# Pairwise products of every row: one form of VectorE instruction, inputs loaded in a ring, and four longer output pieces in place of five

## The chip, the core and the metric

The kernel runs on one core of one Trainium2 chip. The metric is the device time of one execution in microseconds. TensorE has no work here: VectorE and ScalarE multiply, and the 16 DMA engines of the core bring the input in from device memory and write the output back.

## The reference

For each of 4096 rows of 256 float32 numbers, the reference forms all products of two elements of the row and keeps the upper triangle, diagonal included, in row order: 256 + 255 + ... + 1 = 32,896 products.

```python
dot = jnp.einsum('bi,bj->bij', inputs, inputs)
iu, ju = jnp.triu_indices(d)
return dot[:, iu, ju]
```

The input is 4.19 MB, the output 539 MB. One output row is a run of segments: segment i holds element i times elements i to 255, and is 256 - i long.

## The kernel before

Each of the 128 partitions holds 32 rows of the input. The loop over `groups` (16 rounds, index `g`) takes `REPEAT` = 2 rows per partition at a time. Each round's 32,896 output columns are cut by `even_borders` into `PIECES` = 5 pieces of 6528 or 6592 columns. A piece is computed into a slot `o` of the pool `opool`, which has three slots of 2 x 6592 floats per partition, and is then written out by one transfer on the SyncE queue (line 164), in packets of one row of a piece: 6592 floats, 26,368 bytes, two for each partition. A new piece can be computed into a slot only when the transfer that read it has landed.

The very first piece of the kernel is cut further, at `FIRST` = 512, 1536 and 3584 columns, so that output can begin early: it goes out as four transfers.

The input is loaded at the start into one tile `xt` that stays for the whole kernel (line 120), in three transfers of 256, 1792 and 2048 KB (line 124).

Inside a piece, `runs` lists the segments that lie in it. `split` gives the first `k` of them to ScalarE, as one activation (line 137) for each segment and each of the two rows, with the scale read from the input; it stops when VectorE's estimated time for the rest is within `BUDGET` = 1.08 ns per element of the piece, or when ScalarE would take longer than VectorE. In the first piece the budget is 0, so the two engines share the work evenly. VectorE does the rest in one of three ways that `vector_ops` chooses by estimated cost:

- "each": one tensor_scalar per row (line 149), at 130 ns + 0.52 ns per element, twice;
- "all": one tensor_tensor over both rows (line 158), with the scalar operand repeated by a stride of 0;
- "two": one tensor_tensor over both rows and two neighbouring segments. The second segment is one element shorter than the first, so this instruction writes one column too many, which the next segment then overwrites. The input tile has one spare element at its end, cleared by a memset, for reads that run over.

```python
each = REPEAT * (130 + 0.52 * n)
together = 68 + 1.046 * REPEAT * n - (34 if two else 0)
```

`interleave` orders VectorE's instructions of a piece so that they come alternately from its two halves, and `vector_time` adds up the estimates. The Tile layer adds the semaphores and decides the order in which instructions stand on each engine. All transfers, loads and outputs, are issued from one queue, SyncE's, in that order.

Of the kernel before, what the change touches and what calls it, by code (L numbers as in the profile page):

```python
# [1 line left out]

# [4 lines left out]

F32 = mybir.dt.float32
AF = mybir.ActivationFunctionType
ALU = mybir.AluOpType  # L10

P = 128
UNIT = 64
REPEAT = 2
PIECES = 5
BUDGET = 1.08
FIRST = [512, 1536, 3584]


def even_borders(lo: int, hi: int, pieces: int) -> list[int]:  # L20
    units = (hi - lo) // UNIT
    return [lo + units * c // pieces * UNIT for c in range(pieces)] + [hi]


def runs(d: int, lo: int, hi: int) -> list:


    found, at = [], 0
    for i in range(d):
        a, b = max(at, lo), min(at + d - i, hi)  # L30
        if a < b:
            found.append((i, i + a - at, a, b - a))
        at += d - i
    return found


def vector_ops(block: list) -> list:

    ops, k = [], 0
    while k < len(block):
        i, j, at, n = block[k]
        two = k + 2 < len(block) and i == j
        each = REPEAT * (130 + 0.52 * n)
        together = 68 + 1.046 * REPEAT * n - (34 if two else 0)
        if each <= together:
            ops.append(("each", block[k]))  # L50
        elif two:
            ops.append(("two", block[k]))
            k += 1
        else:
            ops.append(("all", block[k]))
        k += 1
    return ops


def interleave(block: list) -> list:  # L60


    half = len(block)
    while half and len(vector_ops(block[:half])) > len(vector_ops(block[half:])):
        half -= 1
    a, b = vector_ops(block[:half]), vector_ops(block[half:])
    return [op for k in range(max(len(a), len(b))) for ops in (a, b) for op in ops[k : k + 1]]


def vector_time(block: list) -> float:  # L70
    t = 0.0
    for way, (i, j, at, n) in vector_ops(block):
        if way == "each":
            t += REPEAT * (130 + 0.52 * n)
        else:
            t += 68 + 1.046 * REPEAT * n * (2 if way == "two" else 1)
    return t


def split(block: list, budget: float) -> int:  # L80


    scalar, k = 0.0, 0
    while k < len(block):
        scalar += REPEAT * (184 + 0.837 * block[k][3])
        if vector_time(block[k:]) <= budget or scalar > vector_time(block[k + 1 :]):
            break
        k += 1
    return k


def window(ap: bass.AP, free: list) -> bass.AP:
    return bass.AP(ap.tensor, ap.offset, [list(ap.ap[0]), *free])


@with_exitstack
def kernel(
    ctx: ExitStack, tc: tile.TileContext, x: bass.AP, out: bass.AP
):

    nc = tc.nc
    n, d = x.shape
    width = out.shape[1]
    assert n % (P * REPEAT) == 0 and width == d * (d + 1) // 2 and width % UNIT == 0
    groups = n // (P * REPEAT)
    borders = even_borders(0, width, PIECES)
    slot = max(b - a for a, b in zip(borders, borders[1:]))  # L110

    xpool = ctx.enter_context(tc.tile_pool(name="x", bufs=1))
    opool = ctx.enter_context(tc.tile_pool(name="o", bufs=3))

    x_in = x.rearrange("(p r) d -> p (r d)", p=P)
    x_out = out.rearrange("(p g r) c -> g p r c", p=P, r=REPEAT)


    total = n // P * d
    xt = xpool.tile([P, total + 1], F32, name="x")  # L120
    nc.vector.memset(xt[:, total:], 0.0)  # L121
    cuts = [0, REPEAT * d, total // 2, total]
    for a, b in zip(cuts, cuts[1:]):
        nc.sync.dma_start(xt[:, a:b], x_in[:, a:b])

    for g in range(groups):
        for c, (lo, hi) in enumerate(zip(borders, borders[1:])):
            o = opool.tile([P, REPEAT, slot], F32, tag="o", name=f"o_{g}_{c}")
            first = g == c == 0
            cuts = [lo, *(FIRST if first else []), hi]  # L130
            for a, b in zip(cuts, cuts[1:]):
                block = runs(d, a, b)
                k = split(block, 0.0 if first else BUDGET * REPEAT * (b - a))
                for i, j, at, length in block[:k]:
                    for r in range(REPEAT):
                        row = (g * REPEAT + r) * d
                        nc.scalar.activation(  # L137
                            o[:, r, at - lo : at - lo + length],
                            xt[:, row + j : row + j + length],
                            AF.Copy,  # L140
                            scale=xt[:, row + i : row + i + 1],
                        )
                row = g * REPEAT * d
                for way, (i, j, at, length) in interleave(block[k:]):
                    at -= lo
                    if way == "each":
                        for r in range(REPEAT):
                            row_r = row + r * d
                            nc.vector.tensor_scalar(  # L149
                                o[:, r, at : at + length],  # L150
                                xt[:, row_r + j : row_r + j + length],
                                xt[:, row_r + i : row_r + i + 1],
                                None,
                                ALU.mult,
                            )
                        continue
                    m = 2 if way == "two" else 1
                    nc.vector.tensor_tensor(  # L158
                        o[:, :, at : at + m * length],
                        window(xt[:, row + j :], [[d, REPEAT], [1, m], [1, length]]),  # L160
                        window(xt[:, row + i :], [[d, REPEAT], [1, m], [0, length]]),
                        ALU.mult,
                    )
                nc.sync.dma_start(x_out[g][:, :, a:b], o[:, :, a - lo : b - lo])  # L164


# [1 line left out]
_INS = ["r_inputs"]  # L168
_OUTS = [((4096, 32896), "float32")]


# [20 lines left out]
```

## Time and profile before

The median of three runs is 1277.83 us (1277.81 to 1277.97). The profiled execution has a span of 1276.1 us from its first to its last instruction.

| What | Value |
|---|---|
| VectorE busy | 1128.9 us, 88% of the span |
| ScalarE busy | 234.7 us, 18% |
| tensor_tensor, line 158 | 1651 instructions, 804.2 us, mean 559 ns |
| tensor_scalar, line 149 | 1326 instructions, 344.9 us, mean 333 ns |
| activation, line 137 | 786 instructions, 233.4 us, mean 384 ns |
| DMA packets | 23,040, mean 426 GB/s over the span |
| memory read, written | 4.19 MB, 538.97 MB |
| an output transfer, issue to landing | 33.0 us (median of 64 of 6592 KB) |

How to read it: busy times are those of one engine and overlap with those of the others. The duration of an instruction reaches into that of the next on VectorE, so a stretch of back-to-back instructions is shorter than the sum of their durations; where a text speaks of a pitch, it means the time from one start to the next. "Issue to landing" counts from the instruction on the queue until all 16 DMA engines have reported; with other transfers ahead in the queue it is longer than the transfer itself. The page counts 1376 of the packets under 512 bytes: these are the 16 semaphore writes of each of the 86 transfers. In views of windows, the DMA share is the time of all packets over 16 times the window, and may pass 1 where packets overlap.

### The profile page before, as it was taken

To read this page: it belongs to the slowest core of one execution; us is meant where nothing else is said; L and a number is where in the kernel's file an instruction comes from. 1 tells how busy PE (TensorE), PEld (TensorE's weight loads), DVE (VectorE), ACT (ScalarE), POOL (GpSimd) and SP (SyncE) were. 2 spreads that over 40 slices of the span, in tenths; PEclk is the share of its full clock that TensorE was granted. 3 is DMA by queue.
4 is the path that set the end of the run, shared out by engine and by line. 5 is a ranking of instruction groups with operands and counts; after the bars stand their busy time and mean duration, and the time that the engine had idled before them with its cause. 6 is when DMAs were issued, how large, how long until landed. Compare 5 with 4: busy or idle time off the path is not lost.

```text
span 1276.1 us, 4106 instructions
## 1 busy us (share of the span) xinstructions
DVE 1128.9 (88%) x2978; ACT 234.7 (18%) x787; POOL 0.2 (0%) x4
## 2 busy tenths in 40 slices
DVE  8999989898898988989889898898988989888880
ACT  4211112121121301213012130121301213012130
POOL 0000000000000000000000000000000000000000
DMA  9999999999999999999999999999999999999997
GB/s 385 433 434 430 428 432 426 433 426 433 428 430 432 427 434 423 435 426 432 428 430 431 427 435 424 434 425 434 429 430 432 426 433 424 434 428 432 430 428 314
DMA packets 23040, 543.43 MB, mean 426 GB/s; under 512 B 1376, under 2 KB 1376, under 8 KB 2016
## 3 DMA queue, kind: packets, MB, share of 16 engines
q1 hardware_dynamic: 23008, 543.17, 99.5%
q14 instruction: 32, 0.26, 0.0%
HBM read 4.19 MB, written 538.97 MB: 426 GB/s over the span
## 4 chain that ended last, share of the span: by engine, by line
DMA 62%; DVE 35%; issue 0%; DVEq 0%; SPq 0%
DMA out_dram<-o 62%; DVE o L158 24%; DVE o L149 11%; DMA x<-in_r_inputs_dram 0%; SPq L164 0%; DVEq L158 0%; DVEq L149 0%; DVEq L188 0%
## 5 line engine op out<-in xcount | busy, mean ns | idle before, releaser
L158 DVE TENSOR_TENSOR o<-x 128x104 f32<-128x104 f32 (+60 forms) x1651 | 804.2, 559 | 59.3 <-DMA out_dram<-o 59.3
L137 ACT ACTIVATE o<-x 128x197 f32<-128x197 f32 (+25 forms) x786 | 233.4, 384 | 1000.6 <-DMA out_dram<-o 892.5
L149 DVE TENSOR_SCALAR o<-x 128x216 f32<-128x216 f32 (+5 forms) x1326 | 344.9, 333 | 53.1 <-DMA out_dram<-o 50.4
L137 ACT ACT_TABLE_LOAD x1 | 1.3, 1283 | 0.7 <-PEq L179 0.7
L121 DVE MEMSET x<- 128x1 f32 x1 | 0.1, 59 | 0.8 <-PEq L179 0.8
L179 POOL MEMSET const-bfloat16-1.0<- 128x1 bf16 x1 | 0.1, 102 | 0.0
L179 POOL MEMSET const-uint8-127<- 128x1 uint8 x1 | 0.1, 102 | 0.0
L179 POOL MEMSET const-float32-0.0<- 128x1 f32 x1 | 0.1, 99 | 0.2 <-issue 0.2
L179 POOL MEMSET const-float32-1.0<- 128x1 f32 x1 | 0.1, 99 | 0.0
## 6 DMA issues: line engine op xcount, KB each, us to landing
out_dram<-o SPq DMA_DIRECT2D x64, 6592.0 KB, 33.0
out_dram<-o SPq DMA_DIRECT2D x15, 6528.0 KB, 33.3
out_dram<-o SPq DMA_DIRECT2D x1, 2944.0 KB, 16.8
x<-in_r_inputs_dram SPq DMA_DIRECT2D x1, 2048.0 KB, 12.6
out_dram<-o SPq DMA_DIRECT2D x1, 2048.0 KB, 13.8
x<-in_r_inputs_dram SPq DMA_DIRECT2D x1, 1792.0 KB, 7.1
out_dram<-o SPq DMA_DIRECT2D x1, 1024.0 KB, 11.8
out_dram<-o SPq DMA_DIRECT2D x1, 512.0 KB, 10.8
```

Of the source, the lines that this page charges most:

```text
L121: nc.vector.memset(xt[:, total:], 0.0)
L137: nc.scalar.activation(o[:, r, at - lo : at - lo + length], xt[:, row + j : row + j + length], AF.Copy, scale=xt[:, row + i : row + i + 1],)
L149: nc.vector.tensor_scalar(o[:, r, at : at + length], xt[:, row_r + j : row_r + j + length], xt[:, row_r + i : row_r + i + 1], None, ALU.mult,)
L158: nc.vector.tensor_tensor(o[:, :, at : at + m * length], window(xt[:, row + j :], [[d, REPEAT], [1, m], [1, length]]), window(xt[:, row + ...
L179: nc = _bacc.Bacc("TRN2", target_bir_lowering=False, num_devices=1)
```

## The change

Three things are changed together.

1. VectorE uses tensor_tensor only. `vector_ops` no longer weighs the three ways: two neighbouring segments are taken together wherever they have their full length in the piece, a single segment otherwise. `BUDGET` goes from 1.08 to 0.95, so `split` gives ScalarE more segments: 1420 activations in place of 786.
2. The input comes in a ring of three small tiles. Each holds `LOADED` = 2 rounds (1024 floats per partition, 512 KB in all, and the spare element, now cleared on GpSimd). Two tiles are asked for ahead of the loop, and each later one four rounds before it is used; the third of them has a buffer free from the start, and in the built program its load stands on the queue ahead of all outputs.
3. The memory this frees (32 KB per partition for the whole input against 12 KB for the ring) goes into longer slots: `PIECES` goes from 5 to 4, pieces have 8192 or 8256 columns, and packets 32,768 or 33,024 bytes.

```diff
-PIECES = 5
-BUDGET = 1.08
+PIECES = 4
+BUDGET = 0.95
+LOADED = 2
 FIRST = [512, 1536, 3584]
...
         i, j, at, n = block[k]
-        two = k + 2 < len(block) and i == j
-        each = REPEAT * (130 + 0.52 * n)
-        together = 68 + 1.046 * REPEAT * n - (34 if two else 0)
-        if each <= together:
-            ops.append(("each", block[k]))
...
+        m = 2 if k + 2 < len(block) and i == j else 1
+        ops.append((block[k], m))
+        k += m
     return ops
...
-    xpool = ctx.enter_context(tc.tile_pool(name="x", bufs=1))
+    xpool = ctx.enter_context(tc.tile_pool(name="x", bufs=3))
...
-    total = n // P * d
-    xt = xpool.tile([P, total + 1], F32, name="x")
-    nc.vector.memset(xt[:, total:], 0.0)
-    cuts = [0, REPEAT * d, total // 2, total]
-    for a, b in zip(cuts, cuts[1:]):
-        nc.sync.dma_start(xt[:, a:b], x_in[:, a:b])
+    def load(g: int):
+        size = LOADED * REPEAT * d
+        xt = xpool.tile([P, size + 1], F32, tag="x", name=f"x_{g}")
+        nc.gpsimd.memset(xt[:, size:], 0.0)
+        cuts = [0, REPEAT * d, size] if g == 0 else [0, size]
+        for a, b in zip(cuts, cuts[1:]):
+            nc.sync.dma_start(xt[:, a:b], x_in[:, g * REPEAT * d + a : g * REPEAT * d + b])
+        return xt
+
+    loaded = {g: load(g) for g in range(0, 2 * LOADED, LOADED)}
...
                 nc.sync.dma_start(x_out[g][:, :, a:b], o[:, :, a - lo : b - lo])
+            ahead = g + 2 * LOADED
+            if c == 0 and g % LOADED == 0 and ahead < groups:
+                loaded[ahead] = load(ahead)
```

## The prediction

> **What bounds the kernel now.** I read the page's parts 1 to 3 first, then the chain of waits, then windows over the last ten and the first thirty microseconds.
>
> ```profile
> DVE 1128.9 (88%) x2978; ACT 234.7 (18%) x787; POOL 0.2 (0%) x4
> ...
> DMA  9999999999999999999999999999999999999997
> ...
> q1 hardware_dynamic: 23008, 543.17, 99.5%
> q14 instruction: 32, 0.26, 0.0%
> ```
>
> The DMA row is full in every slice but the last, and the output queue is busy for 99.5% of the span: this kernel writes at the speed of its DMA engines. VectorE, at 88%, waits for them. The chain in order of time says the same:
>
> ```profile
> 613.59 13.87 DVE o L149 x54
> 627.48 33.31 DMA out_dram<-o
> 660.81 14.22 DVE o L158 x24
> ```
>
> VectorE fills a slot in about 14 us, and the transfer then takes 33 us to land, since two others stand ahead of it. Three slots turn once in 47.3 us. The chain passes 187.87 us and 1181.29 us in the same phase, 63 transfers apart: 15.768 us a transfer, on the slowest of the 16 engines. The windows at the end show that it is one engine:
>
> ```profile
> 1266.00:1267.00 1.00, 0.00 (x0) 0.00 (x0) 0.00 (x0) 1.00 0.98 422
> 1267.00:1268.00 1.00, 0.00 (x0) 0.00 (x0) 0.00 (x0) 1.00 0.25 106
> 1268.00:1269.00 1.00, 0.00 (x0) 0.00 (x0) 0.00 (x0) 1.00 0.18 79
> 1269.00:1274.00 5.00, 0.00 (x0) 0.00 (x0) 0.00 (x0) 1.00 0.06 26
> ```
>
> The last two columns are the DMA share and GB/s. A share of 0.06 is one engine of 16: most have finished near 1267.2, one works until about 1274.8. It is late by some 7 us, after the same number of output packets as the others. The row q14 explains it: 32 instruction fetches of 8 KB. In the window from 18 to 21 us, where packets of 8 KB ran alone, share 1.02 at 431 GB/s gives 16 x 8192 x 1.02 / 431 = 310 ns a packet. VectorE's 3049 instructions (semaphore steps included) at 64 bytes (0.26 MB over 4106) are 23.8 fetches, 7.4 us. I read this as VectorE's stream being fetched through one DMA engine, which therefore ends last.
>
> Finally the start:
>
> ```profile
> 3.60 10.01 ACT L137 ACTIVATE o<-x 128x253 f32<-128x253 f32 x28 [1.59 <-DMA x<-in_r_inputs_dram]
> 3.60 1.14 DVE L149 TENSOR_SCALAR o<-x 128x256 f32<-128x256 f32 x4 [2.74 <-DMA x<-in_r_inputs_dram]
> ```
> ```profile
> 6.00:9.00 3.00, 3.00 (x14) 3.00 (x10) 0.00 (x0) 1.00 0.99 424
> 9.00:12.00 3.00, 3.00 (x14) 3.00 (x11) 0.00 (x0) 1.00 1.13 355
> 12.00:14.00 2.00, 2.00 (x10) 1.61 (x5) 0.00 (x0) 1.00 0.70 257
> ```
>
> The DMA engines are busy with the 4.19 MB of input until about 13.5 us, and behind that wait output parts computed meanwhile. The load hides the start of the computation.
>
> [...] the timeline shows 0.245 us for 224 elements (17.57 to 18.06 for two) and 0.96 us for 856 (16.61 to 17.57). With its larger fixed part tensor_scalar thus costs 1.09 ns per element at this length and tensor_tensor 1.12: VectorE loses little by the exchange. [...]
>
> **The change part by part.**
>
> *Fewer, longer packets.* 83 output transfers become 67, of 16 packets per engine each: 1328 packets per engine become 1072. Price of a packet: at 27.2 bytes/ns the mean 26,317 bytes take 967.5 ns; 15.768 us / 16 is 985.5, so 18 ns are extra. Of these, 7 us / 1264 packets = 5.5 ns belong to the fetches. That leaves 12.5 ns for every packet (if part grows with bytes, 9 to 10). Saving: 256 x 12.5 = 3.2 us, at least 2.2.
>
> *VectorE by tensor_tensor only.* 3049 VectorE instructions become 1881, so 14.7 fetches instead of 23.8 on the engine that ends last: 9.1 x 0.31 = 2.8 us. ScalarE goes from 786 to 1420 activations, 11.7 fetches on, I take it, another engine, still fewer than VectorE's. In the steady state a piece costs VectorE at most 15.7 us (the code's 68 ns + 1.046 ns per element; on the block of 12,244 elements before, 14.1 by that formula against 14.19 in the chain) and ScalarE at most 12.4, while its transfer takes 16 x 1.227 = 19.6. With three slots the next output is issued some 20 us before it is needed, so both hide.
>
> *One interleaving.* The built order puts the last eight instructions of piece 3 of the first round among those of the next piece, behind a wait for the transfer of piece 1. By my times that landed before VectorE arrives there; piece 3 is issued near 67 us, needed at 72. Nothing.
>
> *The ring of loads.* Only three loads (1.5 MB, 3.7 us) stand at the head of the queue; the five others (4 KB packets) follow the outputs. The memsets on GpSimd wait for readers long done. So the start is no longer hidden. VectorE's blocks until piece 1 is finished, by the formula and the built order: 1.27 + 1.89 + 3.03 + 6.38 + 15.46 = 28.0 us. From 3.60 that is 31.6, issued at 31.8 (VectorE is the slower of the two in each block). First packet 1.0 us after the issue (the first load: issued at 0.73, bytes from 1.7); I take 1.1: 32.9. Until then the engines have 3.7 us of loads and 19.8 us of output parts (16 packets each of 2, 4, 8 and 18 KB: 84, 160, 310 and 686 ns), and begin at 1.75: they stand idle for 32.9 - 1.75 - 23.5 = 7.6 us in all, the longest stretch, over 4 us, just ahead of piece 1. Before, the same sum for piece 1 gives an issue at 27.5, with transfers queued to about 29.5: no gap.
>
> *The sum, from piece 1 on, for the slowest engine.* 512 packets of 33,024 bytes at 1226.6 ns = 628.0; 496 of 32,768 at 1217.2 = 603.7; 40 of 4 KB loads at 163 ns = 6.5, and I add 0.5 for going between reads and writes; 14.3 fetches at 0.30 = 4.3. From 32.9 this ends at 1275.9. The same sum for before (29.8 + 79 x 15.768) ends at 1275.4 where the trace has about 1274.8, so I take 0.5 off: 1275.4, that is 0.6 later than before. **The saving of packets and fetches (6 us) and what the slow bulk load cost (about 1.5) are given back at the start (7.6) and in mid-stream loads.** 1277.8 + 0.7 = 1278.5 us.
>
> **Unknown costs.** The switch between reading and writing is not in the trace of before. From below nothing (a fetch of 8 KB mid-stream, also a read, costs only its own length, 7 us / 23.8 = 0.29); from above: the bulk loads ran at 355 GB/s with one dip to 0.70 over 2 us, so 0.6 us each, 3 in all. The latency from issue to first packet: 0.9 to 1.5. The part of the packet overhead that grows with length: up to 1 us.
>
> **Rivals.**
> 1. *Slower*: mid-stream loads at their upper price, or packets over 32 KB that are cut in two (512 more at 12.5 ns, 6 us): 1281 to 1285. For it: no such packet or load is in this trace. Against: cost per packet is the same from 8 to 26 KB. Chance 0.22.
> 2. *Faster*: the start is hidden after all or the fetches weigh more than I think: without the 7.6 us, 1271; with half of it, 1274.7. For it: the ring brings compute no later than before. Against: the engines have only 3.7 us of loads, and VectorE needs 28 us for what they carry in 23.5. Chance 0.08.
> 3. *VectorE becomes the bound*: 15.7 of work and about 1.5 of landing and issue per slot against 19.6; it would need 3 us more in every piece. It would give 64 x 20 = 1280 at the least. Chance under 0.02, counted within rival 1.
>
> My forecast, no measurable change, has 0.70: it holds from 1275.3 to 1280.4. The range reaches from 2.7 us below (all price errors in favour) to 4.1 above (loads at their upper price and 1 us of longer packets).
>
> **What would show it.** A DMA row with a dip in the slices before 33 us and VectorE busy there; piece 1 issued at 31.8; steady transfers of 19.5 to 19.7 us; a lone engine at the end for 4 to 5 us instead of 7; about 28 fetches in q14 (14.7 for VectorE, 11.7 for ScalarE, the rest for the others) and 19,550 packets in all. It is wrong if the first slices are full, if the transfer takes over 19.8 us, if packets number well over 19,600, or if the outputs behind the mid-stream loads come late by more than the loads' 1.3 us.

## The result and the profile after

The changed kernel takes 1282.75 us (median of four runs, 1282.58 to 1282.82) against 1277.9 us before: a ratio of 1.0038, with a 95% interval of 1.002 to 1.0055. It is 4.9 us slower. No change had been forecast, at 1278.5 us.

The page after, its VectorE row, DMA row, queues and loads:

```profile
DVE 990.4 (77%) x1811; ACT 464.6 (36%) x1421; POOL 0.9 (0%) x12
...
DMA  7999999999999999999999999999999999999996
...
DMA packets 19548, 543.40 MB, mean 424 GB/s; under 512 B 1216, under 2 KB 1216, under 8 KB 2880
...
q1 hardware_dynamic: 19520, 543.17, 98.9%
q14 instruction: 28, 0.23, 0.0%
...
x<-in_r_inputs_dram SPq DMA_DIRECT2D x7, 512.0 KB, 44.7
```

VectorE fell from 88% to 77%. The packets fell from 23,040 to 19,548 and the fetches from 32 to 28, both as worked out beforehand. The first digit of the DMA row is 7 where it was 9. Windows over the start and the end of the same kernel (the last two columns are the DMA share and GB/s; a window counts a packet with its whole length where the packet starts, which is why a share can pass 1):

```profile
24.00:28.00 4.00, 4.00 (x6) 0.00 (x0) 0.00 (x0) 1.00 1.03 442
28.00:32.40 4.40, 4.40 (x9) 2.63 (x9) 0.00 (x0) 1.00 0.03 10
32.40:36.00 3.60, 3.60 (x7) 3.60 (x14) 0.00 (x0) 1.00 1.03 440
1264.00:1270.00 6.00, 0.00 (x0) 0.00 (x0) 0.00 (x0) 1.00 1.01 435
1270.00:1274.00 4.00, 0.00 (x0) 0.00 (x0) 0.00 (x0) 1.00 0.17 74
1274.00:1279.00 5.00, 0.00 (x0) 0.00 (x0) 0.00 (x0) 1.00 0.09 40
```

Two things stand out. Between 28.0 and 32.4 us hardly a packet starts while VectorE works through piece 1, whose output is issued at 31.71: the gap that was forecast. And the end is not what was forecast: some three engines of 16 (a share of 0.17), then one or two (0.09), work alone for 9 us, from 1270 to 1279; before, it was one engine for about 6 or 7. The trace also keeps a record of every single packet, with its start, length and size. By these records 13 engines land their last output by 1270.7 us, and the other three at 1273.1, 1277.4 and 1279.3; before, the last engine landed at 1274.8 and the one ahead of it at 1269.3.

The chain of waits of the changed kernel, over three turns of the three slots (start, duration, what):

```profile
271.32 15.88 DVE o L138 x54
...
330.38 15.59 DVE o L138 x24
...
346.02 45.32 DMA out_dram<-o
...
391.44 15.55 DVE o L138 x19
...
450.50 9.70 DVE o L138 x9
```

The turns take 59.06, 61.06 and 59.06 us. The second holds a later load of 512 KB, and it is 2.0 us longer. The forecast had put a later load at 1.4, and had named outputs that come late by more than a load's 1.3 us as a sign of being wrong.

### The profile page after: what moved, and what is told of

Read it like the earlier page. It is cut to its first block, busy times and chain, and to the rows that moved or that the text cites. A ratio compares the mean times of both kernels' runs of the same rounds, so it can differ in the third digit from the quotient of the medians.

```text
span 1280.8 us, 3569 instructions
## 1 busy us (share of the span) xinstructions
DVE 990.4 (77%) x1811; ACT 464.6 (36%) x1421; POOL 0.9 (0%) x12
## 2 busy tenths in 40 slices
DMA packets 19548, 543.40 MB, mean 424 GB/s; under 512 B 1216, under 2 KB 1216, under 8 KB 2880
## 3 DMA queue, kind: packets, MB, share of 16 engines
q1 hardware_dynamic: 19520, 543.17, 98.9%
## 4 chain that ended last, share of the span: by engine, by line
DMA 65%; DVE 31%; issue 0%; DVEq 0%; SPq 0%
DMA out_dram<-o 65%; DVE o L138 31%; DMA x<-in_r_inputs_dram 0%; DVEq L138 0%; SPq L144 0%; DVEq L171 0%
## 5 line engine op out<-in xcount | busy, mean ns | idle before, releaser
L138 DVE TENSOR_TENSOR o<-x 128x512 f32<-128x512 f32 (+62 forms) x1811 | 990.4, 627 | 246.1 <-DMA out_dram<-o 242.6
L129 ACT ACTIVATE o<-x 128x173 f32<-128x173 f32 (+41 forms) x1420 | 463.3, 417 | 767.9 <-DMA out_dram<-o 749.0
```

The costliest lines, as they stand in the source:

```text
L129: nc.scalar.activation(o[:, r, at - lo : at - lo + length], xt[:, row + j : row + j + length], AF.Copy, scale=xt[:, row + i : row + i + 1],)
L138: nc.vector.tensor_tensor(o[:, :, at : at + m * length], window(xt[:, row + j :], [[d, REPEAT], [1, m], [1, length]]), window(xt[:, row + ...
```

## The experiments

All times are medians; the kernel before stood at 1277.9 us in every comparison.

**tensor_tensor alone.** Five pieces and the whole load stay.

```diff
 PIECES = 5
-BUDGET = 1.08
+BUDGET = 0.95
...
+        m = 2 if k + 2 < len(block) and i == j else 1
+        ops.append((block[k], m))
```

> The kernel before with one part of the change alone: VectorE by tensor_tensor only and the budget of 0.95; five pieces and the whole input loaded at the start stay. VectorE's instructions fall from 3049 to 1899, so its stream takes 14.8 fetches instead of 23.8. As the prediction priced it (0.31 us a fetch): 1277.9 - 2.8 = 1275.1 us. By the theory formed on the trace after the change (the engine that ends last loses about 0.65 us with each fetch, since the output packets around it are held up too): 1277.9 - 5.9 = 1272.0 us. If fetches do not set the end: 1277.9.

Measured: 1274.74 us, ratio 0.9975 (0.9965 to 0.9985). The 3.2 us are the prediction's 2.8, not the 5.9 of the theory read off the trace. The window near its end:

```profile
1268.00:1271.00 3.00, 0.00 (x0) 0.00 (x0) 0.00 (x0) 1.00 0.10 44
```

Fewer fetches leave 3 to 5 us of lone work where there were 7. A share of 0.10 is now one to two engines, which fits ScalarE's stream (12.8 fetches by its instructions) being nearly as long as VectorE's (14.8).

**The ring alone.**

```diff
-    xpool = ctx.enter_context(tc.tile_pool(name="x", bufs=1))
+    xpool = ctx.enter_context(tc.tile_pool(name="x", bufs=3))
...
+    loaded = {g: load(g) for g in range(0, 2 * LOADED, LOADED)}
...
+                loaded[ahead] = load(ahead)
```

> The kernel before with the ring of loads alone; five pieces and VectorE's three forms stay. Piece 1 can start some 1.2 us earlier than before, since its compute is done at 27.5 and nothing queues ahead; five later loads go into the stream. With the prediction's 1.4 us per later load: 1277.9 - 1.2 + 7.0 = 1283.7 us. With the 2.05 us that the trace after shows for a later load and 0.2 us more on the late engine: 1277.9 - 1.2 + 11.2 = 1287.9 us. If the ring costs nothing: 1277.9 or less.

Measured: 1288.28 us, ratio 1.0081 (1.0066 to 1.0096). The ring costs 10.4 us by itself, more than the whole change, and close to the second theory's 1287.9. Of the three parts it is the one that loses: tensor_tensor alone gains, and so do four pieces with the whole load, below.

**Piece 1 shared evenly.**

```diff
-                k = split(block, 0.0 if first else BUDGET * REPEAT * (b - a))
+                k = split(block, 0.0 if even else BUDGET * REPEAT * (b - a))
```

with `even = g == 0 and c < 2`.

> The changed kernel with piece 1 of the first round shared evenly between ScalarE and VectorE, as piece 0 is. If the stretch in which the DMA engines stand idle ahead of piece 1 (about 4 us) is lost for good, the time falls by 3.5 to 4.3 us, to 1278.5 to 1279.3 us. If the end is set by later things alone, no change: 1282.8 us.

Measured: 1278.99 us, 3.8 less than the changed kernel. The window that was empty is nearly full (share 0.86 for 0.03):

```profile
28.00:32.40 4.40, 4.40 (x8) 4.40 (x16) 0.00 (x0) 1.00 0.86 364
```

So the gap at the start is lost time, and closing this stretch of 4.4 us brings nearly what it lasts.

**No later loads.**

```diff
-                loaded[ahead] = load(ahead)
+                loaded[ahead] = load(ahead) if g == 0 else loaded[ahead % (3 * LOADED)]
```

> The changed kernel with the five later loads left out: from round 6 on it multiplies the rows of the first three tiles again, so those outputs are of other rows. With the prediction's 1.4 us per later load: 1282.75 - 7.0 = 1275.8 us. With 2.05 us and 0.2 us more on the late engine: 1282.75 - 11.2 = 1271.6 us. If they were free beside the outputs: 1282.8 us.

Measured: 1272.08 us. The five later loads cost 1282.75 - 1272.08 = 10.7 us, 2.13 each. Its chain over the same stretch:

```profile
268.85 15.87 DVE o L138 x54
...
328.05 15.59 DVE o L138 x24
...
387.07 15.55 DVE o L138 x19
```

Turns of 59.20 and 59.02 us, with nothing like the 61.06. The lone work at the end also shrinks, to 5 us:

```profile
1264.00:1269.00 5.00, 0.00 (x0) 0.00 (x0) 0.00 (x0) 1.00 0.11 46
```

**More instructions on VectorE, and on GpSimd.** Two kernels that differ only in the engine:

```diff
...
+            for _ in range(16):
+                nc.vector.memset(spare[:, :], 0.0)
...
```

> The changed kernel with 16 memsets of one element per partition added to VectorE's stream in each piece, 1024 in all, which compute nothing that is used. VectorE has some 3.8 us to spare per piece and they take about 1.2. Its stream takes 22.7 fetches instead of 14.7. If VectorE's fetches fall on the engine that ends last: 8 x 0.31 = 2.5 us more, 1285.2 us, at the price that the run with tensor_tensor alone confirmed; 8 x 0.65 = 5.2 us more, 1288 us, if the late engine can no longer catch up once later loads have pulled the engines apart. If fetches don't matter: 1282.8.

Measured: 1318.37 us, which neither theory foresaw, and which says nothing on fetches. Nothing bound the memsets to their piece, and the Tile layer gathered them: one stretch of the timeline has 62 of them in 7.7 us. The DMA row shows the transfers starved in the first third of the run:

```profile
DMA  7999998788797999999999999999999999999998
```

The memsets bound to their piece, below, answer the question; GpSimd's come first.

> The same 1024 memsets on GpSimd's stream instead: 8.3 fetches there instead of 0.3. If each engine's stream is fetched by a DMA engine of its own, that one stays ahead of the one that fetches VectorE's 14.7, and the time stays at 1282.8 us. If every fetch holds up the same DMA engine, or all of them: as with the memsets on VectorE, 1285.2 to 1288 us.

Measured: 1282.22 us, no longer than the changed kernel. Eight more fetches in GpSimd's stream do not lengthen it. They were gathered in the first 160 us, and they did hold up a DMA engine: the lone work at the end grows, from a share of 0.17 in the same window to

```profile
1270.00:1274.00 4.00, 0.00 (x0) 0.00 (x0) 0.00 (x0) 1.00 0.25 107
```

Four engines now land late, at 1276.2, 1276.7, 1277.2 and 1279.0 us, where there were three. I read this as GpSimd's stream being fetched through another DMA engine than VectorE's, one that is late too, but ends before 1279.0.

**The same count on VectorE, bound to its piece.** From round 1 on, on an element of the slot that VectorE writes afterwards, in the changed kernel (17 a piece) and in the one with tensor_tensor alone (14 a piece):

```diff
+            for _ in range(17 if g else 0):
+                nc.vector.memset(o[:, 1, hi - lo - 1 : hi - lo], 0.0)
```

> The changed kernel with 17 memsets of one element, which VectorE overwrites later in the same piece, ahead of each piece from round 1 on: 1020 in all, now bound to their piece, so that they can't be moved together. VectorE's stream takes 22.7 fetches instead of 14.7. At 0.31 us: 1285.2 us; at 0.65 us, if the late engine can't catch up between fetches while the later loads keep the engines apart: 1288 us; 1282.8 us if fetches don't matter.

Measured: 1286.56 us, 3.8 more for 8.0 fetches: 0.48 us each, between the two prices of 0.31 and 0.65.

> The same addition (14 memsets a piece from round 1 on, 1050 in all) to the kernel with tensor_tensor alone, which has the whole load at the start: 23.0 fetches in VectorE's stream instead of 14.8. If fetches are what the 3.2 us of that run came from, they go again: 1274.7 + 8.2 x 0.31 to 0.39 = 1277.3 to 1277.9 us. If it was the form of the instruction (tensor_scalar slowing transfers), the time stays at 1274.7 us.

Measured: 1277.1 us, 2.4 more for 8.2 fetches: 0.29 us each. Of the 3.2 us that tensor_tensor alone gained, 2.4 go again with instructions that compute nothing, 8.2 fetches for the 9.0 that were saved, so the gain did come from the shorter instruction stream, and not from the form of the instruction.

**Shorter loads.**

```diff
-LOADED = 2
+LOADED = 1
...
-        cuts = [0, REPEAT * d, size] if g == 0 else [0, size]
+        cuts = [0, size]
```

> The changed kernel with tiles of one round: 3 loads of 256 KB stand ahead of the outputs and 13 come later, in place of 5 of 512 KB. The run without later loads put a later load of 512 KB at 2.1 us, of which 1.3 are its data. If the other 0.84 us are a fixed price of each change from outputs to a load and back: 13 x (0.67 + 0.84) = 19.6 instead of 10.7 us, so 1291.7 us. If they go with the bytes: 13 x 1.07 = 13.9, so 1286 us. If later loads cost their data alone (the prediction): 13 x 0.7 = 9.1 instead of 7.0, so 1284.9 us.

Measured: 1285.27 us. Against no later loads that is 13.2 us for 13 loads of 256 KB, 1.01 each, half of what one of 512 KB costs. A fixed price for each change of direction (1291.7) is out. The time by itself does not part the other two numbers (1286 and 1284.9), but the third counts a load of 512 KB at 1.4 us, which the run without later loads had ruled out. So the price goes with the bytes, as far as two sizes can show it.

**Later loads from ScalarE's queue.**

```diff
+        queue = nc.sync if g <= 2 * LOADED else nc.scalar
         for a, b in zip(cuts, cuts[1:]):
-            nc.sync.dma_start(...)
+            queue.dma_start(...)
```

> The changed kernel with the five later loads issued from ScalarE's queue instead of SyncE's, so that they don't stand in line between outputs. If the 0.84 us per load come from the change within one line: they vanish, 1282.75 - 4.2 = 1278.5 us. If reading between writes costs the same from any queue: 1282.8 us. If each of a load's 8 packets per engine now stops the outputs by itself, as a fetch does (0.35 us beyond its length): 1282.75 + 5 x 8 x 0.35 - 4.2 = 1292.5 us.

Measured: 1278.6 us, 4.15 less than the changed kernel. The five loads now cost 6.5 us, 1.3 each. In its chain,

```profile
270.17 15.88 DVE o L139 x54
...
286.11 44.41 DMA out_dram<-o
...
330.61 15.59 DVE o L139 x24
...
389.63 15.55 DVE o L139 x19
```

the turn with a load takes 60.44 us, 1.2 more than the 59.20 of the same turn without loads; the next, 59.02, is the same in both. What was lost, 0.83 us a load, came from standing in the same queue as the outputs.

The packet records show where it is lost. In the changed kernel the last output packet ahead of a later load takes 2.07 us (median) in place of 1.21, on each engine: 79 output packets of 16,128 take over 1.6 us, for five loads on 16 engines. Two windows of the changed kernel just ahead of the second later load show it. The same bytes start in both, and in the second they take half as long again:

```profile
344.10:345.30 1.20, 1.20 (x4) 0.00 (x0) 0.00 (x0) 1.00 1.01 437
345.30:346.50 1.20, 0.66 (x2) 0.00 (x0) 0.00 (x0) 1.00 1.58 437
```

With loads of 256 KB these packets take 1.65 us. With the loads on ScalarE's queue one packet takes over 1.6 us, and in the runs without later loads, or with short outputs in their place (below), none does.

**Four pieces with the whole load, and three.** In the kernel with tensor_tensor alone, with two slots instead of three to make room, and piece 1 shared evenly:

```diff
-PIECES = 5
+PIECES = 4
...
-    opool = ctx.enter_context(tc.tile_pool(name="o", bufs=3))
+    opool = ctx.enter_context(tc.tile_pool(name="o", bufs=2))
...
```

> Four pieces and tensor_tensor only, as in the changed kernel, but the whole input loaded at the start as before; to fit, the output has two slots instead of three, and piece 1 of the first round is shared evenly. Against the run with tensor_tensor alone (1274.7 us) it has 256 packets per engine less and nothing else on the DMA engines. At the prediction's 12.5 ns a packet: 1271.5 us. At the 5 to 6 ns that the late engine alone seems to lose: 1273.3 us. If longer packets bring nothing: 1274.7. If two slots are too few (VectorE's 15.7 us and about 1.5 of landing and issue against 19.6 of a transfer): over 1280 us.

Measured: 1271.4 us, 3.3 less than with five pieces: 13 ns for each of 256 packets, if all of it is theirs.

> The same with three pieces, packets of 44 KB, a budget of 0.9 and one more cut in the first piece. 240 packets per engine less than with four pieces: at 12.5 ns a packet 3 us less than the run with four pieces and two slots, 1268.5 us if that one gives 1271.5; at 5 to 6 ns 1.3 us less. VectorE needs 19.7 us and some 1.5 for landing and issue, against 26 of a transfer; a gap is possible at the start, which would cost up to 3 us.

Measured: 1268.65 us, ratio 0.9928 (0.9913 to 0.9942): 2.75 us for 240 packets, 11.5 ns each. It beats both kernels. Its page:

```profile
DVE 940.4 (74%) x1729; ACT 531.5 (42%) x1603; POOL 0.2 (0%) x4
...
DMA  9999999999999999999999999999999999999997
...
DMA packets 14604, 543.40 MB, mean 429 GB/s; under 512 B 880, under 2 KB 880, under 8 KB 1520
```

Two slots are enough: the DMA row is full from the first slice.

**Short outputs in place of the later loads,** in the kernel without later loads:

```diff
-                nc.sync.dma_start(x_out[g][:, :, a:b], o[:, :, a - lo : b - lo])
+                short = [a, a + 512, b] if c == 1 and g in (2, 4, 6, 8, 10) else [a, b]
+                for s, e in zip(short, short[1:]):
+                    nc.sync.dma_start(x_out[g][:, :, s:e], o[:, :, s - lo : e - lo])
```

> The kernel without later loads (1272.1 us; from round 6 on its outputs are of other rows), with one piece in each of the five rounds in which a later load stood sent as two transfers, of 512 columns (512 KB, 16 packets of 2 KB per engine) and the rest. No bytes are added, 16 packets per engine each are: 5 x 16 x 12.5 ns = 1.0 us, 1273.1 us, if reading is what made the later loads dear. If any short transfer in the line costs the 0.83 us that a load costs beyond its data: 4.2 us more on top, 1277.3 us.

Measured: 1273.21 us, 1.1 more for 80 packets, 14 ns each: the price of a packet and no more. A short transfer in this line was cheap when it wrote (0.2 us each, all told) and dear when it read (0.83 us beyond its data).

**Both repairs.** Even sharing of piece 1 and the later loads from ScalarE's queue:

> The changed kernel with both repairs, piece 1 shared evenly and the later loads issued from ScalarE's queue. If the two losses are separate they add: 1282.75 - 3.76 - 4.15 = 1274.8 us, 3 us under the kernel before. If one hides behind the other: about 1278.6 us.

Measured: 1274.77 us, ratio 0.9975 (0.9965 to 0.9985), where the sum said 1274.8. The changed kernel so repaired is 3.1 us faster than the one before.

**When the engines end.** The packet records give the time at which each of the 16 DMA engines lands its last output. The first column is the median of the 16, the second the last one, both in us from the start of the span.

| Run | Median engine | Last engine |
|---|---|---|
| before | 1267.3 | 1274.8 |
| tensor_tensor alone | 1267.2 | 1271.6 |
| the same with memsets in VectorE's stream | 1267.2 | 1274.1 |
| four pieces, whole load, two slots | 1265.6 | 1268.2 |
| three pieces | 1261.1 | 1265.5 |
| changed kernel | 1270.4 | 1279.3 |
| the same with bound memsets in VectorE's stream | 1270.4 | 1283.3 |
| the same without later loads | 1264.3 | 1269.1 |
| the same with later loads from ScalarE's queue | 1270.2 | 1275.3 |

Fetches move the last engine and leave the median where it is. If the memsets cost time because VectorE took longer, all engines would be late. The later loads move the median by 6 us from either queue, which is about their data (40 packets of 0.16 us on each engine); what the queue of the outputs adds, 4 us on the last engine, is on the late engines alone.

## Why the prediction was wrong, point by point

*What bounds the kernel* held: the DMA engines (98.9% of their span busy with the queue of loads and outputs), and of these, as I read the runs, the one that fetches VectorE's instructions. More instructions on VectorE make the last engine later (1283.3 us for 1279.3, and 1274.1 for 1271.6), as many on GpSimd do not (1279.0).

*Fewer packets, 3.2 us*: held in the sum. It is 3.3 us in the step from five pieces to four with no later loads (13 ns a packet, forecast 12.5), and 11.5 and 14 ns in two other runs. The 27.2 bytes/ns from which the price was worked out stand in the packet records of before: 84 ns (median) for 2 KB and 611 for 16 KB, 14,336 bytes more in 527 ns. Engine by engine the agreement is partly luck: the median engine ends 1.6 us earlier in the first step and 4.5 in the second, that is 6 and 19 ns a packet, and the late engine's distance from it makes up the rest.

*Fewer fetches, 2.8 us*: the number held where the load stands at the start (3.2 us for the part alone; 0.29 us a fetch on the way back, forecast 0.31), but not for the reason given, and so in part by luck. The prediction has a fetch cost "only its own length". In the packet records one in VectorE's stream takes 0.31 us, and the output packet behind it 0.35 us longer than usual (1.57 us for 1.22), in the trace of before as well (1.33 for 0.98). That sets the engine back by 0.66 us. Where no later loads stand in the queue it regains some of this with each transfer (in the run without them the median engine needs 19.55 us for one, the late engine 19.43 where no fetch falls). Between the later loads of the changed kernel the median engine needs 19.43 too, and the late one, at 19.39 where no fetch falls, regains hardly anything; there a fetch costs 0.48. This account is read off the records and was not tested by itself.

*The start, 7.6 us idle*: held where it counts. Piece 1 was issued at 31.71 us for 31.8, and its first packet starts at 32.6 for 32.9: 0.9 us from issue to packet, where 1.1 was put. The longest idle stretch was foreseen at over 4 us; the trace has 4.4, and closing it brought 3.8. By the packet records the engines idle for about 6 us in all, not 7.6, since the loads and first outputs took 24.7 us (mean of the engines) for 23.5.

*Interleaving, VectorE's and ScalarE's longer work*: nothing, as forecast. In the changed kernel's chain VectorE's longest block takes 15.9 us, where a transfer takes 19.4 to 19.6. The 1.5 us of landing and issue per slot was an estimate; the trace after has 1.3, the 0.9 above and 0.4 from the end of the last packet (1279.3 us) to its landing (1279.7). After the start no run made VectorE the bound except the one in which the added memsets were gathered.

*The later loads: here the prediction failed.* It put "40 of 4 KB loads at 163 ns = 6.5, and I add 0.5 for going between reads and writes", 7.0 us in all. The upper bound for going between reads and writes was "0.6 us each, 3 in all". The loads cost 10.7 us. Of this, 6.5 are the data, as forecast (the run from the other queue), and 4.2 come from reading in the queue of the outputs, 0.83 us for each load, where 0.1 was put. The bound was taken from two wrong places. The first is the instruction fetches, which the page lists as a queue of their own (q14), and which in truth cost their engine twice their own length (0.66 us for 0.31). The second is the bulk load, which had no output ahead of it.

Each later load stretches a packet on all 16 engines (2.07 us for 1.21), but by the end most have made up for it: their median is within 0.2 us of that of the run from ScalarE's queue (1270.4 and 1270.2). The last engine has not (1279.3 and 1275.3). So the 4.2 us, and the higher price of a fetch in this kernel, are in part the same loss seen from two sides and must not be added. Whether later loads would cost more than their data if no engine were late was not run.

From ScalarE's queue, too, the load's packets (0.16 us) stand between output packets (1.21 us), and yet the same five loads cost 10.7 us from one queue and 6.5 from the other.

Without the later loads the forecast reads 1278.5 - 7.0 = 1271.5 us, and the kernel without them takes 1272.1. The 3.7 us on this one term carry the time just out of the range (1278.5 + 4.1 = 1282.6), whose upper end was built on the same bound. The rival that named it ("mid-stream loads at their upper price") had the right cause with a chance of 0.22; its other half, packets cut at 32 KB, did not happen (19,548 packets for 19,550).

The measured steps in order: 1277.9, less 3.2 for tensor_tensor, less 3.3 for four pieces, plus 0.7 for a start with three tiles and no later loads (which carries 2.6 MB less and has the idle start), plus 10.7 for the later loads: 1282.8. Each step is the difference of two runs, so the sum has to close; it shows the sizes and proves nothing by itself.

## What to carry to other kernels

Where the DMA engines are the bound, price every transfer by the queue that it stands in and what stands around it, not only by its bytes: here a read of 512 KB put between outputs, in their queue, cost 2.13 us where its data took 1.3. The whole load at the start stood ahead of the outputs, beside the first computation, and with four pieces that kernel took 1271.4 us; before a load is cut up to save memory, look for the room elsewhere (here two output slots did what three did). And when one DMA engine ends late, look at what else it carries: here 8 fetches more or less in VectorE's stream were worth 2.4 to 3.8 us, with VectorE busy for only 77% of the span.

## What the runs showed of the hardware that had not been expected

- Five reads of 512 KB between writes: 2.13 us each from the queue of the outputs, 1.3 from another. The excess goes with the bytes (0.83 us for 512 KB, about 0.35 for 256 KB if the data takes 0.67), and a 512 KB output in the same place shows none of it. It stands in the last output packet ahead of the load, 2.07 us for 1.21. What in the DMA engines holds that packet up stays open.
- In the changed kernel the issue of a load takes 1259 ns (median) on SyncE's queue, and 366 ns on ScalarE's. SyncE waits for VectorE for some 18 us before each output, and with loads of half the size, which lose half as much, the issue takes as long (1258 ns), so the issue time does not set the loss.
- GpSimd's instruction fetches, 8 more of them, do not lengthen the run, while as many in VectorE's stream cost 2.4 to 3.8 us. In the first case a fourth DMA engine becomes late (1276 to 1277 us) and the last one stays at 1279: I read this as the two streams not being fetched by one and the same DMA engine.
- A fetch of 8 KB in VectorE's stream takes 0.31 us on its DMA engine, and the output packet behind it 0.35 us longer than usual (1.57 us for 1.22 in the changed kernel).
- A packet more or less costs 11.5 to 14 ns of the whole time in three runs. The records of undisturbed packets have a fixed part of 8 ns: 159 ns for 4 KB and 309 for 8 KB in the trace of before, 1213 for 32 KB in that of after.
